# Mamba's weights and phi's fold set among the first experts' blocks, and the opening of Mamba in an order of its own

## The chip, the core and the metric

The kernel is one program on one core of a Trainium2 chip. The metric is device time of one execution in microseconds (us), the median of several runs. PE is TensorE (PEld its weight loads), DVE is VectorE, ACT ScalarE, POOL GpSimd, SP SyncE, which here only issues DMAs.

## The reference

Two layers work on an activation x of 4 x 1024 tokens with 128 features, all in fp32. A layer norm stands ahead of every part, and every part's result is added to x.

```
x = x0                                   # 4 x 1024 x 128
x += MoE(LN(x))                          # 8 experts, top 2, hidden 512, 1024 places each; half weight
x += Mamba(LN(x))                        # inner 256, state 16, causal conv of 4 taps
x += MoE(LN(x))                          # the same experts again; half weight
x += SoftMoE(LN(x))                      # 64 experts x 32 slots, logits x @ phi.T + phi_b
x += GLA(LN(x))                          # 16 heads of 8, gated linear attention
x += SoftMoE(LN(x))

Mamba:  u, z  = split(x @ W_in);   uc = silu(conv4(u) + conv_b)
        dt, B, C = split(uc @ W_xproj)
        delta = softplus(dt @ W_dt + b_dt)
        h_t = exp(-delta_t exp(A_log)) * h_(t-1) + delta_t B_t uc_t
        out = ((sum_n C_t h_t + D uc) * silu(z)) @ W_out
```

## The kernel before

Tokens lie on 128 partitions in 32 tiles of 128 tokens; a "tile group" is four of them, 512 tokens. The stages follow one another:

- **Front and routing** (`front`, `moe_routes`): x is loaded in eight DMAs on SP, each tile group gets its layer norm (DVE statistics, a power on POOL, then `nmr` on DVE), is transposed, and its normed rows `xn_d` go to HBM. DVE ranks the experts and works out each slot's token, `src`, and each result's place, `dest`. SP then loads the experts' weights w1, w2, b2 and clears `y2_d`, the place of results, in HBM (4 MB).
- **First experts** (`moe_experts`): 64 chunks of 128 slots in 16 blocks of four. POOL issues an indirect gather for each chunk, four blocks ahead, and an indirect scatter of each result (L405, L411). For a block, PE transposes (`turn`), multiplies by w1 (`hidden`, ACT evicts with Relu) and by w2 (`output`, DVE evicts to `eo`). The order is written out by hand: `turn(blk + 2)`, `hidden(blk + 1)`, gathers and scatters, `output(blk)`. When no gather is left, POOL does a small memset in its place ("spacer").
- **The fold of phi** (`soft_weights`, L878 to L915), for the much later soft experts: for each of four quarters of phi, ACT squares it, PE sums the squares over the partitions (`pn`) and spreads phi's last row (`pr`), DVE takes the greatest sum and subtracts. Then phi's bias is transposed, its bounds are tested (`flag`), and its negative is put in phi's last row by way of HBM. Here `ones` is a memset on POOL.
- **Opening of Mamba** (`mamba_layer`): weights w_in, w_x, w_dt, w_out and cw (the conv's taps, multiplied into w_in by DVE) are loaded on ACT's queue; A and dg are made. Then come the first half row (512 tokens) of Mamba by `prologue`, and, mixed into it, the results of the first experts by `combine`: for each tile group y is brought from `y2_d` by SP, ACT scales the first choice (L502), DVE multiplies the second and adds x (L494), adds both (L512), and takes the layer norm's statistics (L124, L125, L128), POOL the power (L138), DVE `nmr` (L145). `prologue` transposes the normed tiles (xn, L201; pt, L597), copies them (xT, L599), does the conv and projection as 128x512 matmuls (pu, L618 and L624), evicts (uc, L609; zs, L613), applies Silu to both, projects again (pp, L636; dbc, L641), and makes delta and du (L656 to L680). dbc's rows B and C go by HBM (`bc_d`) to all partitions.
- **Mamba's units**: 8 half rows x 16 states, each a decay on ACT, scans on DVE, products on POOL and sums on PE, in an order by hand. Then the second routing (its constants, `tri_f` to `keep` in `moe_routes`, are made by POOL whenever its memory is free), the second experts with the same code, soft experts, GLA, soft experts.

Within `tc.manual_schedule(engines=ENGINES)` the order on PE, DVE, ACT and POOL is that of the code; SP's and everything outside is placed by a scheduler. Each engine runs its queue in order. `combine` mixes a tile group's pieces into `prologue` three at a time, each group in one go:

```
others = (_ for j in range(4, NT, 4) for _ in pieces(j, wk))
for _ in prologue(*halves[0], rs[0], psa, "dA"):
    for _ in range(3):
        next(others, None)
```

Of the kernel before, what the change touches and what calls it, by code (L numbers as in the profile page):

```python
# [18 lines left out]
P = 128  # L19
B, S, D = 4, 1024, 128  # L20
T = B * S
# [50 lines left out]
def macaron_kernel(ctx: ExitStack, tc: tile.TileContext, a: dict, out: bass.AP):  # L72
# [319 lines left out]
    def moe_experts(w1, w2, b2, tag, xn_d, src, dest):  # L392

        with ExitStack() as s1:
# [64 lines left out]
            with tc.manual_schedule(engines=ENGINES):  # L459
                for c in range(AHEAD * 4):  # L460
                    gather(c)
                turn(0)
                turn(1)
                hidden(0)
                for blk in range(NBLK + 1):
                    if blk + 2 < NBLK:
                        turn(blk + 2)
                    if blk + 1 < NBLK:
                        hidden(blk + 1)
                    for i in range(4):  # L470
                        c = (blk + AHEAD) * 4 + i
                        if c < NSB:
                            gather(c)
                        elif blk > 0:
                            nc.gpsimd.memset(spacer, 0.0)
                        if blk > 0:
                            scatter((blk - 1) * 4 + i)
                    if blk < NBLK:
                        output(blk)

# [49 lines left out]

    def run(pieces):
        for _ in pieces:
            pass


    def mamba_layer(ln, ln_next, first, route, rxp):
# [5 lines left out]
        with ExitStack() as s:  # L542
# [10 lines left out]
            w_in = load("w_in", [D, 2 * DI], wp)  # L553
            w_x = load("w_x", [P, NC, XO[2] + DS], wp)
            w_dt = load("w_dt", [DR, DI], wp)
            w_out = load("w_out", [P, NC, D], wp)
            cw = wp.tile([P, DC, DI], F32, name="cw")
            nc.scalar.dma_start(
                out=cw.rearrange("p k c -> p (k c)"), in_=a["conv_wT"].partition_broadcast(P)
            )  # L560

            for k in range(DC):
                nc.vector.tensor_tensor(cw[:, k, :], cw[:, k, :], w_in[:, :DI], ALU.mult)

            def col(name, c):
                i = COLS[name].start + c
                return cols[:, i : i + 1]

            A = wp.tile([P, NC * DS], F32, name="A")
            nc.scalar.activation(A, cols[:, COLS["A_log"]], AF.Exp)  # L570
            nc.vector.tensor_scalar(A, A, -1.0, None, ALU.mult)
            dg = wp.tile([P, NC, P], F32, name="dg")
            for c in range(NC):
                nc.vector.tensor_scalar(dg[:, c, :], ident, col("D", c), None, ALU.mult)
# [6 lines left out]
            def prologue(b, h, r, ps=ps, tag="mm"):  # L581
# [102 lines left out]
                yield  # L684

# [131 lines left out]
            with tc.manual_schedule(engines=ENGINES):  # L817
                bring, pieces = first
                for j in range(0, 16, 4):
                    bring(j, wk)  # L820
                run(pieces(0, wk))


                others = (_ for j in range(4, NT, 4) for _ in pieces(j, wk))
                for _ in prologue(*halves[0], rs[0], psa, "dA"):
                    for _ in range(3):
                        next(others, None)
                run(others)
                for k in range(3):
                    at(fetch, k)  # L830
                at(feed, 0)
                at(feed, 1)
                at(decay, 0)
                at(decay, 1)
                LEAD = 5
                ahead, old, behind = (iter(()) for _ in range(3))
                for k in range(-LEAD, len(units) + 7):
                    if k % DS == DS - LEAD and (k + LEAD) // DS + 1 < len(rs):
                        i = (k + LEAD) // DS + 1
                        old, ahead = ahead, prologue(*halves[i], rs[i])  # L840
                    if k < 0:
                        next(ahead, None)
                        continue
                    if k > DS and k % DS == 2:
                        behind = epilogue(rs[k // DS - 1])
                    at(fetch, k + 3)
                    at(scan, k)
                    late = next(behind, None)
                    at(keep, k)
                    at(decay, k + 2)  # L850
                    at(times_c, k - 1)
                    at(feed, k + 2)
                    at(sums, k - 2)
                    if late:
                        next(behind)
                    next(old, None)
                    next(ahead, None)
                run(behind)
                route.top_two(NT - NJ, NJ)

# [6 lines left out]
    def soft_weights(pool):  # L867
# [3 lines left out]
        phiN = load("phiT", [D, NS], pool)  # L871
        pbc = pool.tile([P, NSC], F32, name="pbc")
        flag = pool.tile([1, 1], I32, name="flag")
        with (
            tc.tile_pool(name="fold", bufs=2) as wk,
            tc.tile_pool(name="foldp", bufs=2, space=PSUM) as ps,
        ):
            pb = wk.tile([NSC, P], F32, name="pb", bufs=1)  # L878
            nc.scalar.dma_start(out=pb, in_=a["phib"].rearrange("(c p) -> c p", p=P))
            ones = wk.tile([P, P], F32, name="ones", bufs=1)  # L880
            nc.gpsimd.memset(ones, 1.0)
            n2 = wk.tile([P, NS // 512], F32, name="n2", bufs=1)
            for q in range(NS // 512):
                qs = slice(q * 512, (q + 1) * 512)
                sq = wk.tile([P, 512], F32, name="sq")
                nc.scalar.activation(sq, phiN[:, qs], AF.Square)
                pn = ps.tile([P, 512], F32, name="pn")
                nc.tensor.matmul(pn, ones, sq, start=True, stop=True)
                nc.vector.tensor_reduce(n2[:, q : q + 1], pn, AX.X, ALU.max)
                pr = ps.tile([P, 512], F32, name="pr")  # L890
# [4 lines left out]
                nc.vector.tensor_tensor(phiN[:, qs], pr, phiN[:, qs], ALU.subtract)  # L895

            pt = ps.tile([P, 512], F32, name="pt", tag="pn")
            nc.tensor.transpose(pt[:, :NSC], pb, ident[:NSC, :NSC])
            nc.scalar.copy(pbc, pt[:, :NSC])
            ab = wk.tile([P, 1], F32, name="ab", bufs=1)  # L900
# [4 lines left out]
            pc = ps.tile([P, 512], F32, name="pc", tag="pr")  # L905
            nc.tensor.matmul(pc[:, 0:1], ones, ab, start=True, stop=True)
            nm = wk.tile([P, 1], F32, name="nm", bufs=1)
            nc.vector.tensor_reduce(nm, n2, AX.X, ALU.max)
            nc.vector.tensor_scalar(nm, nm, MAX_N2, None, ALU.is_le)
            nc.vector.tensor_tensor(nm, nm, pc[:, 0:1], ALU.add)  # L910
            nc.vector.tensor_scalar(flag, nm[0:1, :], float(P + 1), None, ALU.is_equal)
            nc.scalar.activation(pb, pb, AF.Copy, scale=-1.0)
# [3 lines left out]
        return phiN, pbc, flag  # L916
# [778 lines left out]
    with tc.tile_pool(name="moewa", bufs=1) as wpool:  # L1695
        with tc.tile_pool(name="rtmpa", bufs=1) as tp:
            route = moe_routes("a", tp)
            with (
# [13 lines left out]
                with tc.manual_schedule(engines=ENGINES | {mybir.EngineType.SP}):  # L1712
# [3 lines left out]
                    for j in range(0, NT + 32, 4):  # L1716
# [4 lines left out]
                        if j == NT + 8:  # L1721
                            weights = moe_weights(wpool)
                            clear()
                        if j == NT + 8:
# [3 lines left out]
        moe_experts(*weights, "a", route.xn_d, src, dest)  # L1728

    spool = ctx.enter_context(tc.tile_pool(name="softw", bufs=1, side="right"))  # L1730
    phiN, pbc, flag = soft_weights(spool)
    with tc.tile_pool(name="rtmpb", bufs=1, side="right") as tp:
        route = moe_routes("b", tp)
        with tc.tile_pool(name="rxb", bufs=1) as rxp:
            mamba_layer(lns[1], lns[2], combine(gates[0], lns[1], 4, "hst"), route, rxp)
# [3 lines left out]


# [117 lines left out]
```

## Time and profile before

| what | us |
|---|---|
| median of 3 runs | 2222.7 |
| lowest and highest run | 2218.91, 2224.62 |
| the profiled execution | 2225.24 |
| its span, first to last instruction | 2223.5 |
| front and routing, to the first gather | 0 to 66.1 |
| first experts, to the end of the last scatter | 66.1 to 230.9 |
| opening of Mamba, to du of the first half row | 230.9 to 288.9 |
| Mamba, second routing, to the first gather | 288.9 to 846.6 |

Busy over the whole span: PE 1919.8 us (86%), DVE 1397.4 (63%), ACT 952.3 (43%), POOL 1399.0 (63%). The mean granted clock of PE is 0.927 of full speed. A row of the timeline gives start, duration, engine, line, operation, output<-inputs, size, and in brackets the idle time of the engine before it and what ended that. A row of a table by stage gives the stage's bounds and length, each engine's busy time and count, the granted clock as a share of full speed, the share of time that the DMA engines were busy, and GB/s.

### The profile page before, as it was taken

Reading aid. Unit: us, or ns where it says so; the run is one execution under the profiler, and the core shown is the slowest. Engines: PE = TensorE matmul, PEld = TensorE weight load, DVE = VectorE, ACT = ScalarE, POOL = GpSimd, SP = SyncE. Lnnn points to the kernel's source line nnn. Section 1 sums busy time; section 2 is a strip of 40 time slices with the busy share of each in tenths; the row PEclk is TensorE's granted clock in tenths of the full one; section 3 lists DMA queues with packets and bytes.
Section 4 is the critical chain, followed back from the end, with each engine's and each line's share of the span. In section 5 each row is a group of like instructions: output and inputs, shape, how many; then the busy total and the mean of one; then the engine's idle time right before and its main releaser. Section 6 shows DMA issues by size and latency. Waiting matters only on the chain. (4 is left out here: it accounts for less than half of the span.)

```text
span 2223.5 us, 18016 instructions
## 1 busy us (share of the span) xinstructions
PE 1919.8 (86%) x5893; PEld 892.6 (40%) x5893; DVE 1397.4 (63%) x1839; ACT 952.3 (43%) x1595; POOL 1399.0 (63%) x919
## 2 busy tenths in 40 slices
PE   5788578888999866885999989997888999989998
PEld 3556223333334324653444444443223344434443
DVE  6211678888888982115888645566976788744445
ACT  4322466677776623222443343332542333333331
POOL 3677278898988946775555566662543455556663
PEclk9999789999899876997999999998987999999999
DMA  7111433332332324112000000000000000000000
GB/s 248 49 52 50 143 107 98 107 117 101 124 105 98 116 95 129 52 51 63 19 10 0 1 1 1 0 1 6 1 0 1 1 0 1 1 1 5 10 10 16
DMA packets 63389, 110.70 MB, mean 50 GB/s; under 512 B 7967, under 2 KB 41391, under 8 KB 58293
## 3 DMA queue, kind: packets, MB, share of 16 engines
q1 hardware_dynamic: 53222, 85.04, 11.6%
q0 software_dynamic: 8192, 16.79, 2.7%
q10 hardware_dynamic: 1874, 7.65, 1.0%
q8 instruction: 48, 0.79, 0.2%
q14 instruction: 53, 0.43, 0.1%
HBM read 90.00 MB, written 19.44 MB: 49 GB/s over the span
## 5 line engine op out<-in xcount | busy, mean ns | idle before, releaser
L1017 POOL TENSOR_TENSOR dm<-ex,sm 128x1024 f32<-128x1024 f32 x128 | 247.8, 1936 | 215.2 <-DVE sm L1013 109.1
L758 POOL TENSOR_TENSOR hc<-hst,Cs 128x1024 f32<-128x1024 f32 x127 | 280.9, 2220 | 55.2 <-DVE hst L741 24.9
L1125 POOL TENSOR_TENSOR acc<-acc,L 128x1024 f32<-128x1024 f32 x96 | 226.0, 2355 | 116.6 <-ACT L L1117 115.9
L773 PE MATMUL py<-hc,ident 128*128 128x512 f32 x512 | 278.1, 674 | 17.6 <-POOL hc L758 17.4
L1117 ACT ACTIVATE L<-pl,pbc 128x512 f32<-128x512 f32 x256 | 162.1, 684 | 283.7 <-PE pl L1107 273.2
L1005 ACT ACTIVATE ex<-l,nmh 128x1024 f32<-128x1024 f32 x128 | 142.7, 1115 | 289.9 <-DVE nmh L1000 269.7
L996 PE MATMUL l<-phiT,xT 128*128 128x512 f32 x512 | 247.8, 608 | 18.8 <-ACT ex L1005 15.6
L1107 PE MATMUL pl<-xT,phiM 128*128 128x512 f32 x512 | 244.7, 603 | 0.1
L1151 PE MATMUL py<-L,yt 128*128 128x512 f32 x512 | 238.4, 593 | 4.4 <-DVE L L1141 4.4
L1028 PE MATMUL px<-dm,xn 128*128 128x512 f32 x512 | 240.8, 593 | 1.1 <-POOL dm L1017 1.1
L1000 DVE TENSOR_REDUCE nmh<-l 128x1 f32<-128x1024 f32 x128 | 156.1, 1220 | 78.8 <-PE l L996 78.2
L731 ACT ACTIVATE dA<-delta,A 128x512 f32<-128x512 f32 x256 | 177.1, 719 | 50.8 <-DVE hst L741 45.7
L437 ACT ACTIVATE hT<-ph,cols 128x512 f32<-128x512 f32 x128 | 88.0, 687 | 216.5 <-PE ph L433 216.5
L723 POOL TENSOR_TENSOR dBu<-du,Bs 128x1024 f32<-128x1024 f32 x78 | 172.5, 2212 | 1.7 <-DVE du L680 1.2
L741 DVE TENSOR_TENSOR_SCAN hst<-dA,carry,dBu 128x512 f32<-128x512 f32 x128 | 155.4, 1264 | 11.8 <-ACT dA L731 6.3
L773 PEld LDWEIGHTS py<-hc,ident 128*128 128x128 f32 x512 | 96.2, 202 | 163.5 <-issue 122.0
L996 PEld LDWEIGHTS l<-phiT,xT 128*128 128x128 f32 x512 | 97.9, 194 | 150.7 <-issue 116.8
L741 DVE TENSOR_TENSOR_SCAN hst<-dA,dBu 128x512 f32<-128x512 f32 x128 | 147.5, 1203 | 16.9 <-POOL dBu L723 8.5
L1012 DVE TENSOR_REDUCE sm<-ex 128x32 f32<-128x1024 f32 x128 | 154.7, 1209 | 0.0
L452 DVE TENSOR_TENSOR eo<-po,b 128x512 f32<-128x512 f32 x32 | 22.1, 692 | 207.6 <-PE po L447 207.6
L411 POOL DMA_INDIRECT y_d<-eo,dest x128 | 126.1, 985 | 40.9 <-issue 25.6
L1151 PEld LDWEIGHTS py<-L,yt 128*128 128x128 f32 x512 | 96.8, 190 | 127.3 <-issue 117.0
(259 smaller groups left out, 3016.6 us busy)
## 6 DMA issues: line engine op xcount, KB each, us to landing
Cs<-bc_d SPq DMA_DIRECT2D x32, 1024.0 KB, 5.9
Bs<-bc_d SPq DMA_DIRECT2D x78, 256.0 KB, 3.1
w<-in_w SPq DMA_DIRECT2D x4, 2048.0 KB, 8.2
y<-y_d SPq DMA_DIRECT2D x32, 256.0 KB, 3.3
y_d<-zero SPq DMA_DIRECT2D x1, 4096.0 KB
ew<-in_ew ACTq DMA_DIRECT2D x1, 4096.0 KB
x<-in_x SPq DMA_DIRECT2D x8, 256.0 KB, 6.9
xn_da<-xr SPq DMA_DIRECT2D x8, 256.0 KB, 4.9
```

What stands on the lines that cost most here:

```text
L723: eng.tensor_tensor(dBu, r["du"], r.pop(("B", n)).unsqueeze(2).to_broadcast([P, HB, NC]), ALU.mult,)
L731: nc.scalar.activation(dA, r["delta"][:, :, c], AF.Exp, scale=A[:, c * DS + n : c * DS + n + 1],)
L741: nc.vector.tensor_tensor_scan(hst[:, :, c], r.pop(("dA", n, c)), dBu[:, :, c], 0.0 if h == 0 else carry[b][:, c, n : n + 1], ALU.mult, AL ...
L758: eng.tensor_tensor(hc, r.pop(("h", n)), Cs.unsqueeze(2).to_broadcast([P, HB, NC]), ALU.mult)
L773: nc.tensor.matmul(r["py"][:, c, :], ident, hc[:, :, c], start=False, stop=(n == DS - 1))
L996: nc.tensor.matmul(l[:, q * 512 : (q + 1) * 512], xT[:, j * P : (j + 1) * P], phiN[:, o : o + 512], start=True, stop=True,)
L1017: nc.gpsimd.tensor_tensor(dms[k], exs.pop(k), sms.pop(k).unsqueeze(2).to_broadcast([P, NG, PS]), ALU.mult,)
L1028: nc.tensor.matmul(px[hf * 2 + q], xns[j // 4][:, j % 4, :], dmf[:, q * 512 : (q + 1) * 512], start=(j == 0), stop=(j == NT - 1),)
L1107: nc.tensor.matmul(pl[:, i, :], phiM[:, (2 * c + i) * P : (2 * c + i + 1) * P], xT[:, t * TB : (t + 1) * TB], start=True, stop=True,)
L1117: nc.scalar.activation(L[:, i, :], pl[:, i, :], AF.Exp, bias=pbc[:, 2 * c + i : 2 * c + i + 1], scale=-1.0,)
L1125: nc.gpsimd.tensor_tensor(accs[t], accs[t], L, ALU.add)
L1151: nc.tensor.matmul(pys[t], yt[:, 2 * c + i, :], L[:, i, :], start=(c + i == 0), stop=(c == CS - 1 and i == 1),)
```

## The change

Three things change, all ahead of Mamba's units.

1. phi and Mamba's weights are loaded by SP right after the clearing of `y2_d` (phi was loaded on ACT's queue at the start of the kernel, Mamba's weights there at its opening). Their tiles have pools of their own on the other side of SBUF. The fold and the making of cw, A and dg become generators, whose pieces `moe_experts` runs one by one after `output(blk)` from block 2 on: four quarters of phi (blocks 2 to 5), the bias and bounds (6), the flag and the row by HBM (7), cw (8), A and dg (9). The fold's PSUM tiles come from the ring of `ph`. `ones` is made by DVE.
2. The first half row has `opening` in place of `prologue`: uc and zs are evicted from PSUM with Silu at once, the second z projection comes after pp, and each step follows the former without empty pieces between.
3. In place of `combine`, `flow` brings the results of the first experts: the scale of the next tile group is issued ahead of the present group's add, and `nmr` of a group comes behind the next group's add. (The second experts' results still use `combine`.)

In the program as built, two more things follow. From du of the first half row on, each engine's order is that of before. The eleven instructions of POOL that make the second routing's constants, which stood behind the first tile group's power, now stand behind the gather of chunk 52 and ahead of the scatter of chunk 32: their pool now shares addresses with the fold's tiles.

```diff
@@ moe_experts
+                others = extra(psh, "ph") if extra else iter(())
                 for blk in range(NBLK + 1):
...
                     if blk < NBLK:
                         output(blk)
+                    if blk >= 2:
+                        next(others, None)
+    def flow(gate, ln, yp, tag):
...
+        def scale(j):
+            if j < NT:
+                for i in range(4):
+                    nc.scalar.activation(
+                        ys[j][:, 0, i, :], ys[j][:, 0, i, :], AF.Copy,
+                        scale=gate[:, 0, j + i : j + i + 1],
+                    )
+        def add(j):
+            y = ys.pop(j)
...
+            bring(j + 16)
+        for j in range(0, 16, 4):
+            bring(j)
+        scale(0)
+        add(0)
+        ln_group(ln, 0)
+        yield
+        scale(4)
+        for j in range(4, NT, 4):
+            scale(j + 4)
+            add(j)
+            yield
+            if j > 4:
+                ln_minus(ln, j - 4)
+            ln_stats(ln, j)
+            ln_pow(ln, j)
+            yield
+        ln_minus(ln, NT - 4)
+    def mamba_weights(wp):
+        w = {
+            "w_in": load("w_in", [D, 2 * DI], wp, nc.sync),
...
+        def pieces():
+            for k in range(DC):
+                nc.vector.tensor_tensor(
+                    cw[:, k, :], cw[:, k, :], w["w_in"][:, :DI], ALU.mult
+                )
+            yield
...
+            def opening(r, ps, tag):
...
+                def project(q):
...
+                        nc.scalar.activation(uc[:, q, :], pu, AF.Silu, bias=col("conv_b", q))
...
+                        nc.scalar.activation(zs[:, q - NC, :], pu, AF.Silu)
+                for q in range(NC + 1):
+                    project(q)
+                    yield
...
+                project(NC + 1)
+                yield
...
-                bring, pieces = first
-                for j in range(0, 16, 4):
-                    bring(j, wk)
-                run(pieces(0, wk))
-                others = (_ for j in range(4, NT, 4) for _ in pieces(j, wk))
-                for _ in prologue(*halves[0], rs[0], psa, "dA"):
-                    for _ in range(3):
+                others = first(wk, "hst")
+                next(others)
+                for i, _ in enumerate(opening(rs[0], psa, "dA")):
+                    next(others, None)
+                    if i % 2:
                         next(others, None)
                 run(others)
@@ soft_weights
-        phiN = load("phiT", [D, NS], pool)
+        phiN = load("phiT", [D, NS], pool, nc.sync)
...
-            nc.gpsimd.memset(ones, 1.0)
+            nc.vector.memset(ones, 1.0)
...
@@ macaron_kernel
+    spool = ctx.enter_context(tc.tile_pool(name="softw", bufs=1, side="right"))
+    mpool = ctx.enter_context(ExitStack())
+    mwp = mpool.enter_context(tc.tile_pool(name="mwts", bufs=1, side="right"))
+    with (
+        tc.tile_pool(name="moewa", bufs=1) as wpool,
+        tc.tile_pool(name="fold", bufs=1, side="right") as fp,
+    ):
...
                             clear()
+                            phiN, pbc, flag, fold = soft_weights(spool)
+                            mweights, made = mamba_weights(mwp)
...
+        def extra(ps, tag):
+            yield from fold(fp, ps, tag)
+            yield from made()
+        moe_experts(*weights, "a", route.xn_d, src, dest, extra)
```

## The prediction

> **What bounds the kernel now.** I read the table by stage first, to see which stage the change touches and what limits it.
>
> ```profile
> core 0: us, PE busy (x) PEld busy (x) DVE busy (x) ACT busy (x) POOL busy (x), PEclk, DMA share, GB/s
> 0.00:66.00 66.00, 34.24 (x162) 26.09 (x162) 41.26 (x140) 25.61 (x60) 22.08 (x49) 1.00 0.62 216
> 66.00:231.00 165.00, 136.75 (x710) 93.23 (x710) 23.15 (x34) 45.13 (x66) 127.37 (x149) 0.95 0.18 51
> 231.00:290.00 59.00, 27.26 (x47) 10.29 (x47) 41.03 (x144) 31.72 (x64) 10.32 (x13) 0.64 0.52 162
> ```
>
> Stage 66 to 231 is the first experts, 231 to 290 the opening of Mamba. In the opening no engine is full: it is a chain of waits. In the experts' stage POOL shows 127 of 165 us, but the timeline of POOL has it issuing gathers and scatters from 66.14 to 230.87 with nothing but 0.3 us between two of them (and one hole of 1.1 at 211), one every 1.28 us. POOL sets that stage's end; ACT and DVE are mostly idle there, and PE waits 24.8 us for gathers. The timeline around the change:
>
> ```profile
> 8.21 0.29 DVE L124 BATCH_NORM_STATS2 st<-x 128x6 f32<-128x128 f32 x1 [0.81 <-DMA x<-in_x]
> ...
> 229.90 0.97 POOL L411 DMA_INDIRECT y_d<-eo,dest  x1 [0.19 <-issue]
> ...
> 232.16 2.59 SPq L491 DMA_DIRECT2D y<-y_d  x5
> ...
> 244.71 0.16 DVE L145 SCALAR_TENSOR_TENSOR nmr<-mv,rstd 128x4 f32<-128x4 f32 x1 [1.16 <-POOL rstd L138]
> ...
> 248.80 0.56 ACT L599 COPY xT<-pt 128x512 f32<-128x512 f32 x1
> ...
> 258.41 0.69 ACT L609 ACTIVATE uc<-pu,cols 128x512 f32<-128x512 f32 x1 [1.58 <-PE pu L618]
> ...
> 287.61 1.26 DVE L680 TENSOR_TENSOR du<-delta,uc 128x1024 f32<-128x1024 f32 x1
> ```
>
> Call S the start of the last scatter, 229.90. From S the opening reaches its marks at +14.8 (first tile group's nmr), +18.9 (xT copy), +28.5 (second uc), +57.7 (du). From du on, the order of instructions on every engine is the same in both kernels, so what is won up to du is won in the end. The same first steps occur without a fold beside them after the second experts, whose last scatter starts at 1014.45:
>
> ```profile
> 1014.45 0.97 POOL L411 DMA_INDIRECT y_d<-eo,dest  x1 [0.19 <-issue]
> ...
> 1019.79 1.28 ACT L502 ACTIVATE y<-y,gate 128x128 f32<-128x128 f32 x4 [18.14 <-DMA y<-y_d]
> 1020.52 1.14 DVE L494 SCALAR_TENSOR_TENSOR y<-y,gate,x 128x128 f32<-128x128 f32 x4 [10.88 <-DMA y<-y_d]
> ...
> 1025.61 0.16 DVE L145 SCALAR_TENSOR_TENSOR nmr<-mv,rstd 128x4 f32<-128x4 f32 x1 [1.23 <-POOL rstd L138]
> ```
>
> There nmr stands at +11.2 from the scatter, not +14.8. That is my template for the new opening.
>
> **The opening (flow, opening, weights made earlier), step by step from S.**
> nmr +11.2; the first xn 0.2 later, +11.4. ACT still runs eight scales of y (tile groups 4 and 8) behind xn and ahead of the xT copy: 1.55 after xn's start plus 2.34 (246.46 to 248.80 in the row of before) gives the xT copy at +15.3; before +18.9.
> The second uc came 9.6 after the xT copy (258.41 against 248.80); the matmuls between are the same 16 passes: +24.9. I add 0.75 for the clock (below): +25.65. Silu now evicts directly, and its table load (1.28) stands in ACT's queue ahead of the first uc, where ACT waits for PE anyway, so it leaves the path.
> Meanwhile DVE does seven further tile groups without waiting for POOL's power. From rows of one group: four multiply-adds 1.22, add to stats 0.73, stats to eps 1.9, nmr 0.1: 3.9 a group, where before the nmr rows stand 5.05 apart, 1.12 of it idle until POOL's power, as in front of the nmr above. The one place where the new order still stops DVE is the group at 16: its scales (1.26) are behind the second uc on ACT. 25.65 + 0.7 + 1.26 puts that add at +27.7 (DVE alone would be there at +25.9). Three more groups of 3.9: +39.4; last stats 2.7: +42.1; power and nmr 1.3: +43.4; then w, l and delta, 1.25 each (282.16 to 283.41): du at +47.2. ACT's own chain from there: second uc 0.7, four groups of scales 5.0, two Silu evictions 1.4, dbc 0.6, four evictions of pd 2.8 (the 2.15 from dbc to the first of them, 268.62 to 270.78, is filled by scales and a Silu but for 0.2), then 5.9 from the last to the end of Ln (274.44 to 280.35): +42.3, inside DVE's +43.4. B and C fetches start about +31 and have 10 us to spare. Gain of the opening: 57.7 - 47.2 = **10.5 us**.
>
> The clock. In the windows 249:253 and 253:257 the granted clock is 0.50 and 0.99: the first 3.6 us of these matmuls run at half speed, 0.85 a pass for 0.43. After the second experts, where PE had idled longer (no fold before it), the first eight passes all took 0.83 (6.66 us). The fold no longer runs just ahead, so I take 5.1 us at half speed, the middle between 3.6 and 6.7: half of the difference, +0.75. Bounds: 0, and all 16 passes slow, +4.7.
> [...]
>
> **The fold and the weights among the blocks.** Each quarter of phi adds to PE four passes of 0.43 (1.7), to ACT one square (0.63), to DVE 0.69 twice; the first also waits about 1.1 for ones, now a DVE memset behind eo. The small rest, cw (4 x 0.42), A and dg are some 4 us of DVE in all. The cover is POOL's pace: eo of block 2 ends at 106.86 and its scatter goes at 113.29, 6.4 us later; from block 3 on the lead is 9 to 13. The pieces add at most 2.8 + 3 x 1.7 = 8 us to PE by block 5, spread over four blocks, and PE waits 1.5 to 2.5 per block for gathers later, which give it back. I cost them at nothing; without cover they would cost those 8 us.
> POOL's own queue: the set-up of the second routing (tri_f to keep, eleven instructions) was at 7.16 to 9.23, in idle time. Its pool now lies over the fold's tiles, and the order puts it behind the gather of chunk 52 and ahead of scatter 32, near 175 us, where POOL is the bound: **+2.1**. Queued behind it are all later gathers and scatters, so S moves with it. Bounds: 1.0 (the hole at 211 takes up 1.1 of it) and 3.3 (a wait and an issue gap more). Its wait is for the fold's last reads, due about 20 us earlier.
>
> **The loads.** phi (1 MB) left ACT's queue at 1.73 and shared the DMA engines with x; DVE lost 0.81 waiting for the second x group (row above). It now follows w1, w2, b2 and the clearing: **-0.8** (0 to -1), since from there to the first gather it is one chain. The 2 MB moved behind the clearing extend traffic that ended near 57 us by some 5 us at its 400 GB/s, before the first gather at 66. SP has nothing left between scatters and y loads except the flag, read earlier. pb on SP waits for nothing late.
>
> **Sum.** -10.5 + 2.1 - 0.8 = -9.2 us. The profiled execution took 2225.24 us (span 2223.5), so 2216.0 for it; it lies 2.5 above the median of 2222.7, which gives **2213.5 us**.
>
> **Rivals.**
> *The opening wins little* (0.17). PE stays slow through all 16 passes and pp and pd after them, so that ACT's in-order scales hold up DVE at 16, 20 and 24: 4.7 less, and about 1 more at pp. For it: ACT is in order, and a scale stands behind every eviction. Against it: before, the clock rose 3.6 us into the same matmuls. Gain 10.5 - 5.7 = 4.8, less 1.3 net upstream: -3.5, 2219.2.
> *POOL stands still in the middle of the experts* (0.05), the one that ends slower. The set-up's first memset waits for the fold's last read; if phi arrived late (it is behind 8.5 MB), the fold would stall PE at block 2 and POOL at chunk 52. The fold spans blocks 2 to 7, about 46 us (106 to 152). It decides once the wait passes the 9.2 won: the fold would have to end after 184, so phi to land after 138 instead of near 62. If it landed at 150, the fold would end at 196, POOL would wait 21 us, and the time be 2213.5 + 21 = 2234. Against it: DMA is 18% busy in that stage.
> *More is won* (0.10): the hole at 211 swallows half of the set-up (1.1), and the clock rises so early that the scales at 16 come in time (1.8): -12.1, 2210.6.
> The forecast has 0.68.
>
> **Numbers.** By its own bounds (set-up 1.0 to 3.3, x 0 to -1, clock 3.6 to 6.7 us) the forecast spans 2211.5 to 2216.5; for 8 in 10 the range reaches to the two near rivals: 2208.5 to 2219.5. 0.3% is 6.7 us, about what a measurement of this kernel tells from no change: faster means under 2216.0. That takes nearly all of the forecast and of the third rival, 0.76; same 0.19; slower 0.05.
>
> **What would show it.** Right: first gather near 65.3; last scatter near 231.2 with tri_f to keep inside POOL's row near 174; nmr at S + 11.2, xT at S + 15.3, du at S + 47; every later mark 9 earlier. Wrong: S later than 233, a wait in front of tri_f, scatters waiting for eo, granted clock at 0.5 beyond 7 us of pu, or DVE idle in front of more than one add.

## The result, and the profile after

The changed kernel takes **2216.76 us** (median of 20 runs, 2210.57 to 2222.43) against 2223.59 for the kernel before (20 runs beside them, 2218.91 to 2227.32): a ratio of 0.9968, 95% interval 0.9958 to 0.9977, or 6.8 us won, between 5.1 and 9.3. The forecast was 9.2 won; the 6.8 are just past the 6.7 that it named as about the least that can be told from no change. The profiled execution of the changed kernel is one of its slower ones, 2221.28 us with a span of 2219.1, only 4.0 under that of the kernel before. So there are two things to explain: what was won where the change is, and why the end shows less.

One fact is needed for the numbers below: e1 to e4 ran on chip 10 and e9 to e12 on chip 4, and on both every kernel took 40 to 50 us longer (the kernel before: 2269.7 and 2271.7). They are called the long chips here. e5 to e8 ran on chip 9 (the kernel before: 2224.9) and agree with the first two profiles, whose chip is not on record; the chips of these six profiles are called the short chips. Times are compared only within a series; marks are counted from S, the start of the last scatter of the first experts.

The table by stage of the changed kernel, cut at its first gather and its last scatter:

```profile
core 0: us, PE busy (x) PEld busy (x) DVE busy (x) ACT busy (x) POOL busy (x), PEclk, DMA share, GB/s
65.00:231.00 166.00, 135.94 (x723) 93.86 (x723) 29.77 (x54) 46.55 (x71) 128.01 (x158) 0.98 0.18 51
231.00:280.00 49.00, 16.97 (x34) 6.77 (x34) 33.93 (x125) 27.31 (x57) 10.12 (x13) 0.60 0.56 176
```

The experts' stage holds 6.6 us more of DVE and no less of POOL, and is not shorter; the opening has shrunk from 59 to 49 us. The timeline of the changed kernel at the places shown for the kernel before, and at the new ones:

```profile
7.33 0.28 DVE L124 BATCH_NORM_STATS2 st<-x 128x6 f32<-128x128 f32 x1
...
172.51 0.97 POOL L407 DMA_INDIRECT g<-xn_da,src  x1 [0.30 <-issue]
173.48 0.22 POOL masks.py:65 MEMSET tri_f<- 128x128 f32 x1
...
175.40 0.13 POOL L232 MEMSET keep<- 128x8 f32 x1
176.12 1.02 POOL L413 DMA_INDIRECT y_d<-eo,dest  x1 [0.59 <-issue]
...
231.03 0.97 POOL L413 DMA_INDIRECT y_d<-eo,dest  x1 [0.19 <-issue]
...
242.39 0.16 DVE L145 SCALAR_TENSOR_TENSOR nmr<-mv,rstd 128x4 f32<-128x4 f32 x1 [1.16 <-POOL rstd L138]
...
245.44 0.69 DVE L564 TENSOR_TENSOR x<-y 128x512 f32<-128x512 f32 x1 [1.84 <-ACT y L552]
...
246.48 0.56 ACT L769 COPY xT<-pt 128x512 f32<-128x512 f32 x1
...
247.14 9.93 PE L778 MATMUL pu<-xT,cw 128*128 128x512 f32 x16 [2.38 <-ACT xT L769]
...
257.11 0.69 ACT L782 ACTIVATE uc<-pu,cols 128x512 f32<-128x512 f32 x1 [2.75 <-PE pu L778]
...
258.99 0.69 DVE L564 TENSOR_TENSOR x<-y 128x512 f32<-128x512 f32 x1 [2.37 <-ACT y L552]
...
277.84 1.25 DVE L833 TENSOR_TENSOR du<-delta,uc 128x1024 f32<-128x1024 f32 x1
```

DVE no longer waits for x at the start. The set-up of the second routing stands in POOL's row with no wait in front: from the gather at 172.51 to the scatter at 176.12 are 3.61 us instead of 1.28. S is 231.03; nmr comes at S + 11.4, the xT copy at S + 15.45, the second uc at S + 26.1, the add of group 16 at S + 28.0, du at S + 46.8. In the kernel before du stood at S + 57.7. So at du the changed kernel is 9.77 us ahead, and at the end of the span 4.4. From du on both kernels run the same instructions in the same order (but for one last nmr of DVE, which the kernel before has behind du), yet the changed one took 1941.2 us for them and the other 1935.9.

### The profile page after: what moved, and what is told of

Read it like the earlier page. It is cut to its first block, busy times and chain, and to the rows that moved or that the text cites. A ratio compares the mean times of both kernels' runs of the same rounds, so it can differ in the third digit from the quotient of the medians.

```text
span 2219.1 us, 17996 instructions
## 1 busy us (share of the span) xinstructions
PE 1896.7 (85%) x5893; PEld 886.4 (40%) x5893; DVE 1400.1 (63%) x1840; ACT 949.5 (43%) x1593; POOL 1396.3 (63%) x918
## 5 line engine op out<-in xcount | busy, mean ns | idle before, releaser
L1293 DVE TENSOR_TENSOR L<-L,rd 128x1024 f32<-128x1024 f32 x128 | 147.0, 1211 | 0.1
```

## Experiments

The table gathers all profiles; each column is worked out from the starts of the instructions named. "Mamba" is du to the first gather of the second experts, "experts 2" from there to their last scatter, "soft 1" the first to the last pass of l, the soft experts' logits, "GLA" from there to the first pass of l in the second soft experts. "Half" is the time in GLA at half granted clock, by the clock records of the trace.

| profile | first gather | S | S to du | Mamba | experts 2 | soft 1 | GLA | half |
|---|---|---|---|---|---|---|---|---|
| before | 66.14 | 229.90 | 57.71 | 558.96 | 167.88 | 236.06 | 460.34 | 76.0 |
| before, e5 | 65.29 | 228.71 | 56.56 | 558.57 | 167.46 | 236.04 | 456.38 | 57.7 |
| after | 65.20 | 231.03 | 46.81 | 558.21 | 169.45 | 237.36 | 463.89 | 78.9 |
| e6 set-up free | 65.29 | 228.78 | 46.29 | 558.17 | 169.41 | 237.75 | 460.14 | 75.8 |
| e7 scales early | 65.22 | 231.04 | 42.69 | 558.44 | 167.63 | 236.06 | 456.08 | 57.7 |
| e8 warm | 65.21 | 232.02 | 54.28 | 557.76 | 169.81 | 237.75 | 459.95 | 76.0 |
| *chip 10:* e1 after | 65.14 | 254.90 | 45.51 | 557.24 | 191.14 | 236.05 | 457.29 | 69.3 |
| e2 old opening | 65.26 | 254.31 | 54.11 | 557.79 | 190.38 | 237.72 | 459.87 | 76.0 |
| e3 fold behind | 65.30 | 258.63 | 47.12 | 557.48 | 189.94 | 237.74 | 460.13 | 75.9 |
| e4 both repairs | 65.24 | 253.57 | 42.75 | 555.83 | 188.74 | 236.05 | 459.89 | 76.1 |
| *chip 4:* e9 after | 65.30 | 255.17 | 46.64 | 558.38 | 189.87 | 237.35 | 463.08 | 81.5 |
| e10 fold behind | 65.42 | 255.65 | 46.97 | 559.97 | 191.29 | 236.05 | 463.97 | 78.9 |
| e11 both repairs | 65.44 | 253.40 | 43.12 | 557.66 | 189.90 | 237.75 | 457.26 | 69.3 |
| e12 warm, gated | 65.30 | 255.09 | 45.37 | 557.43 | 188.63 | 237.75 | 463.98 | 78.9 |

**Is the loss behind du the kernel's, or the execution's? (e1, e9, e5.)** No edit: the changed kernel twice more, the kernel before once.

> The changed kernel once more, nothing edited. The first profile had du at 277.84, 9.8 us ahead of the kernel before, but the span ended only 4.4 ahead: from du to the end it took 1941.3 us against 1935.9. Theory A (clock windows): what lies behind du is the same instructions, and the loss is the luck of the granted clock, which drops by half for windows of 3.41 us and takes 1.7 us of a TensorE-bound stretch each time. Then first gather, last scatter and du repeat within 0.3 us (65.2, 231.0, 277.8), the stretch from du to the end does not (anything from 1932 to 1944), and the two profiles of this one kernel drift apart behind du in steps near 1.7 us where their clock records differ. Theory B (the new order costs something later): the stretch from du to the end repeats at 1941.3 within 1 us, with the same steps at the same places.

> The changed kernel once more, as the measure for the three others of this call. On a chip like the first: first gather 65.2, S 231.0, du at S + 45.5 to 46.8 (its two profiles), and a stretch from the last pass of the first soft experts to the first pass of the second that lies anywhere from 456 to 464 (463.9 in its first profile, 457.3 in its second, 456.4 to 460.3 in the two of the kernel before): by the theory of clock windows it does not repeat; by the rival (a lasting cost of the new order) it is 463 or more on the chip where it was 463.9.

> The kernel before, nothing edited, for a profile beside those of this call. The chip of the runs e1 to e4 was slower for every kernel (before: 2269.7), by about 24 us in each experts' stage, where TensorE showed gaps of issue between its passes; marks are therefore counted from S, the last scatter. Expected: S to du 57.7 within 1 us, whatever the chip; from du to the end, outside of the second experts' stage, the same as in every other run but for steps of 1.7.

Measured: e1 2259.43 us, ratio 0.9947 (0.9926 to 0.9967); e9 2263.88, 0.9967 (0.9948 to 0.9985); e5 2225.54, 1.0003 (0.9992 to 1.0014). First gather and S to du of the changed kernel repeat within 1.3 us, not within the 0.3 that was expected, and S itself moves with the chip. What follows du does not repeat (e1's 1954.0 from du to the end holds a second experts' stage 21.7 longer). The stretch GLA of the changed kernel took 463.9, 457.3 and 463.1 us, that of the kernel before 460.3 and 456.4, with the same instructions. One row over that stretch, of the first profile and of e1:

```profile
1257.00:1721.00 464.00, 416.46 (x1326) 172.43 (x1324) 296.98 (x372) 176.84 (x289) 242.67 (x124) 0.91 0.00 1
```

```profile
1299.00:1757.00 458.00, 413.36 (x1327) 168.99 (x1326) 295.88 (x373) 177.04 (x289) 242.60 (x124) 0.92 0.00 1
```

DVE, ACT and POOL have the same work to 1.1 us; PE is busy 3.1 us longer at a lower clock. Over the 14 profiles the stretch goes with its time at half clock (the last two columns): 456 us where 57.7 us are at half, 457 at 69.3, 460 to 464 at 76 and above. It is no price list: from 57.7 to 69.3 the stretch grows by 1.1, from 76.0 to 78.9 by 3.8. In the clock records of the first profiles of both kernels every stretch at one clock, but for the last, which the end of the record cuts, is a multiple of 3.41 us long (3.41 to 249.17 us, each at 1.00 or 0.50); 3.41 us are called a window here. The weight loads of pu's passes in the first profile of the changed kernel start 0.85 us apart up to 252.83, where the record has 0.50, and 0.43 apart behind it, where it has 1.00; by these numbers one window at half clock costs a PE that is busy all through it an estimated 1.7 us of work. The stretch soft 1 takes one of three values, 236.05, 237.35 and 237.75. Held against each other instruction by instruction, the first two profiles of the changed kernel drift apart and back between du and the second experts by up to 6.5 us, mostly in steps of 1 to 3, as the first profiles of the two kernels do. Theory B, a fixed loss of GLA, falls with e1's 457.3 and, on the short chips, with the 456.1 of e7, which from du on is the same. Of theory A it is shown that the stretch does not repeat; that the clock is the cause is argued. Which comes first in each place, the longer time or the half clock, the columns do not tell. Two counts even speak against theory A for the whole: from du to the end the first profile of the kernel before has 270 us at half clock and that of the changed one 248, though the latter took longer; and over the 20 runs of the changed kernel, time and mean granted clock do not go together (correlation -0.07). These counts hold half windows in which PE had no work as well, so they are rough.

From the first pair, the 5.3 us lost behind du are: Mamba -0.75, experts 2 +1.57, soft 1 +1.30, GLA +3.55, and -0.3 in the rest. A small lasting cost is not excluded: on the short chips, du to the end took 1935.9 and 1931.5 with the order before (mean 1933.7) and 1941.2, 1937.9, 1931.7 and 1937.4 with the new ones (1937.1).

e5 also shows what the forecast could not see, in the timeline of the kernel before's second profile:

```profile
7.34 0.29 DVE L124 BATCH_NORM_STATS2 st<-x 128x6 f32<-128x128 f32 x1
...
228.71 0.97 POOL L411 DMA_INDIRECT y_d<-eo,dest  x1 [0.19 <-issue]
```

phi's load is still at the front there, and the 0.81 us of waiting for x is not: the first gather is at 65.29.

**Which half of the change won the 10.9? (e2, e3, e10.)** e2 keeps fold and weights among the blocks and takes the old order of the opening (lines shortened):

```
-  lambda yp, tag: flow(gates[0], lns[1], yp, tag)
+  combine(gates[0], lns[1], 4, "hst")
-  others = first(wk, "hst"); next(others)
-  for i, _ in enumerate(opening(rs[0], psa, "dA")):
-      next(others, None)
-      if i % 2: next(others, None)
+  bring, pieces = first
+  for j in range(0, 16, 4): bring(j, wk)
+  run(pieces(0, wk))
+  others = (_ for j in range(4, NT, 4) for _ in pieces(j, wk))
+  for _ in prologue(*halves[0], rs[0], psa, "dA"):
+      for _ in range(3): next(others, None)
```

> Fold and weights stay among the blocks; the opening goes back to the old order (combine and the general prologue). It tells how much of the 10.9 us won between last scatter and du (57.7 to 46.8) is the missing fold and weights, and how much the order. My theory: last scatter S stays at 231.0; first nmr at S + 11.4 instead of S + 14.8, because only the fold and the weights stood in its way; the rest of the old opening is unchanged, so du at S + 54 (285): 3.4 won by moving the fold, 7.2 by the order. Time about 7 us above the changed kernel, near 2224. Rival (the order does nothing, the freed DVE does it all): du at S + 47 to 48, time within 1 us of the changed kernel. Second rival (the fold was hidden behind other waits): nmr S + 14.8, du S + 57.7, time near 2228.

Measured: 2270.13 us, ratio 1.0003 (0.999 to 1.0017): nothing of the gain is left, and the time is 10.7 above e1, where 7 was expected. From its timeline:

```profile
254.31 0.97 POOL L413 DMA_INDIRECT y_d<-eo,dest  x1 [0.19 <-issue]
...
265.52 0.16 DVE L145 SCALAR_TENSOR_TENSOR nmr<-mv,rstd 128x4 f32<-128x4 f32 x1 [1.16 <-POOL rstd L138]
...
272.33 0.16 DVE L145 SCALAR_TENSOR_TENSOR nmr<-mv,rstd 128x4 f32<-128x4 f32 x1 [1.14 <-POOL rstd L138]
...
277.38 0.16 DVE L145 SCALAR_TENSOR_TENSOR nmr<-mv,rstd 128x4 f32<-128x4 f32 x1 [1.12 <-POOL rstd L138]
...
308.42 1.25 DVE L751 TENSOR_TENSOR du<-delta,uc 128x1024 f32<-128x1024 f32 x1
```

nmr at S + 11.2 and du at S + 54.1, both as expected: beside the old order, fold and weights out of the way are worth 3.0 (57.1, the mean of the two profiles of before, less 54.1). Groups still stand 5.05 apart, with 1.12 of waiting for POOL's power in each; in the changed kernel the adds of two groups without a wait stand 3.75 apart. And 3.0 less the 2.25 that POOL's set-up costs (e6, on a short chip) is no gain that these runs can tell.

e3 and e10 are one kernel, the opposite half: the new opening, with phi's fold behind the experts again (shortened).

```
-  moe_experts(*weights, "a", route.xn_d, src, dest, extra)
+  moe_experts(*weights, "a", route.xn_d, src, dest)
+with (tc.tile_pool(name="fold", bufs=1) as fp,
+      tc.tile_pool(name="foldp", bufs=4, space=PSUM) as fps):
+    for _ in extra(fps, "ph"): pass
```

> The opposite half: the new order of the opening stays, but phi's fold and the products of the weights go back behind the experts (the loads stay where the change put them, and POOL's set-up of the second routing is early again, because nothing lies under its tiles). My theory: S at 228.7 (231.0 less the 2.3 of the set-up); DVE, ACT and TensorE have the fold ahead of the first group, so nmr at S + 14.8 and du at S + 50.2 (279): about 1.4 later than in the changed kernel, time near 2218. Rival (the new order has slack that swallows the fold): du at S + 47, time near 2214.5.

> The kernel of e3 again (phi's fold behind the experts, loads and opening as in the changed kernel; the products of the weights are placed early by the scheduler, near 78, as e3 showed). On the slow chip du came at S + 47.1, because fold and first y tile hardly meet: from the end of the experts' last eo DVE, ACT and TensorE wait about 12 for y, and only 1.3 of the fold falls behind y's landing. My theory now: on a chip like the first, S at 228.8 (no set-up in POOL's row), du at S + 47.1, so near 275.9, about 1.5 ahead of the changed kernel: moving the fold among the blocks costs 2.3 on POOL and brings 0.8. Time 1.5 under that of e9, so equal to it by the measurement. Rival (the fold among the blocks is worth the 3 that it brought beside the old order, 57.1 to 54.1): du at S + 49, 278 or later.

Measured: e3 2262.67 us, 0.9964 (0.9949 to 0.998); e10 2262.49, 0.996 (0.9942 to 0.9978), e9 beside it 2263.88. du is at S + 47.1 and S + 47.0, not at S + 50.2: e3's number was a miss by 3, and its rival's (S + 47) came. The timeline of e10 tells why:

```profile
249.31 0.69 DVE L454 TENSOR_TENSOR eo<-po,b 128x512 f32<-128x512 f32 x1 [2.88 <-issue]
...
250.10 0.17 DVE L1029 MEMSET ones<- 128x128 f32 x1
...
251.88 0.69 DVE L1037 TENSOR_REDUCE n<-pn 128x1 f32<-128x512 f32 x1 [1.62 <-issue]
...
255.65 0.97 POOL L413 DMA_INDIRECT y_d<-eo,dest  x1 [0.19 <-issue]
...
257.03 0.69 DVE L1037 TENSOR_REDUCE n<-pn 128x1 f32<-128x512 f32 x1
261.84 0.35 DVE L560 SCALAR_TENSOR_TENSOR y<-y,gate,x 128x128 f32<-128x128 f32 x1 [4.12 <-DMA y<-y_d]
262.11 0.68 DVE L1043 TENSOR_TENSOR phiT<-pr,phiT 128x512 f32<-128x512 f32 x1
```

Between the last eo and the first y DVE has 12 us to wait, and the fold lies in them but for its last 1.3 us. The kernel before has that gap too, from its last eo at 222.56 to its first add of y at 238.96, but there the fold fills the end of it:

```profile
230.87 0.22 POOL L881 MEMSET ones<- 128x128 f32 x1
...
231.15 5.26 PE L888 MATMUL pn<-sq,ones 128*128 128x512 f32 x6 [4.74 <-POOL ones L881]
```

In the kernel before `ones` is a memset of POOL, queued behind the last scatter, so the fold's sums begin at S + 1.25. In e10 DVE makes `ones` right behind the last eo, and they begin at S - 4.9 (250.72). So e3 and e10 put the fold back but not the engine of `ones`, and the fall from 3.0 to 0.7 is not the new order's alone; the kernel before with this one memset moved was not run.

With `ones` on DVE and the new order, then, the fold's move among the blocks brings 0.7 at du (46.3, the mean of after, e1, e9 and e6, against 47.0) and costs 2.25 on POOL. That this half alone would be 1.5 ahead of the whole change on the short chips is worked out from these marks; it was run on the long chips only, where S moves by up to 5 us from profile to profile and the times do not tell it apart. (The products of the weights did not move behind: the scheduler placed them near 78.)

**What does POOL's set-up cost, and what do the scales on ACT? (e6, e7, e4, e11.)** e6 lays the fold's tiles on the other side of SBUF, so that the constants of the second routing no longer wait for them:

```
-        tc.tile_pool(name="fold", bufs=1, side="right") as fp,
+        tc.tile_pool(name="fold", bufs=1) as fp,
```

> The first of the two repairs of e4 alone: POOL makes the constants of the second routing at the start. My theory: the set-up costs 2.3 where POOL's issue of gathers and scatters is the bound. On a chip like that of the first profiles S is at 228.7 (changed kernel 231.0), the time 2.3 lower, near 2214.5. On a chip like that of e1 to e4, POOL waits for eo in front of nine scatters, and the set-up falls into such a wait: S and the time as in the changed kernel, within 1. S to du stays at 45.5 to 47. Rival (the set-up was hidden in the 1.3 us hole before the last scatters): S unchanged on either chip.

Measured: 2211.93 us, 0.9941 (0.9924 to 0.9957). Its timeline:

```profile
7.21 0.20 POOL masks.py:65 MEMSET tri_f<- 128x128 f32 x1
...
228.78 0.97 POOL L413 DMA_INDIRECT y_d<-eo,dest  x1 [0.19 <-issue]
```

These are four runs, and the changed kernel was not run beside them. tri_f is back in POOL's idle time, and S is 2.25 earlier (231.03 in the changed kernel, 231.04 in e7 on the same chip as e6). From first gather to S are 163.5 us, in the two profiles of before 163.76 and 163.42: the fold itself costs the experts nothing on a short chip. What was expected for a long chip was not run alone; in e4 and e11 S is 1.3 and 1.8 ahead of e1 and e9, but e3 and e10, one kernel, have S 3.0 apart there.

e7 issues the scales a tile group earlier, into ACT's wait for the first nmr:

```
         scale(0)
+        scale(4)
+        scale(8)
         add(0)
...
-        scale(4)
         for j in range(4, NT, 4):
-            scale(j + 4)
+            scale(j + 8)
```

> The second repair of e4 alone: scales of y a group earlier on ACT. S as in the changed kernel; S to du 42.8 as in e4 (42.75), 3.3 under the mean of the two profiles of the changed kernel (46.8 and 45.5); no idle of DVE in front of an add. Time about 3 lower than the changed kernel. Rival (part of e4's gain from S to du came from POOL's earlier constants): 45 or more.

Measured: 2210.91 us, 0.9953 (0.9935 to 0.997), again from four runs. Its timeline:

```profile
238.58 1.28 ACT L552 ACTIVATE y<-y,gate 128x128 f32<-128x128 f32 x4 [1.23 <-DMA y<-y_d]
240.78 1.28 ACT L552 ACTIVATE y<-y,gate 128x128 f32<-128x128 f32 x4 [0.92 <-DMA y<-y_d]
242.49 1.65 ACT L201 ACTIVATE xn<-x,nmr,rstd 128x128 f32<-128x128 f32 x4 [0.44 <-DVE nmr L145]
...
243.60 0.69 DVE L564 TENSOR_TENSOR x<-y 128x512 f32<-128x512 f32 x1
...
254.86 0.69 DVE L564 TENSOR_TENSOR x<-y 128x512 f32<-128x512 f32 x1
...
273.73 1.26 DVE L834 TENSOR_TENSOR du<-delta,uc 128x1024 f32<-128x1024 f32 x1
```

Both waits of DVE are gone (the adds of groups 4 and 16, 243.60 and 254.86), and du is at S + 42.7. The add of group 16 stands at S + 23.8. ACT waits 0.92 for y of group 8, and these scales end 0.4 before xn: a landing later by more than that would hold xn.

e4 and e11 carry both edits.

> Two repairs of the changed kernel. One: the fold's tiles lie on the other side of SBUF, not under the constants of the second routing, so POOL makes these constants at the start and not between two scatters: S at 228.7, 2.3 earlier. Two: the scales of the tile groups 4 and 8 are issued in the 4.8 us in which ACT waits for the first nmr, and every later one a group earlier. In the changed kernel the scales behind xn hold the xT copy from S + 13.9 (transposes done) to S + 15.45, and DVE stands 1.84 in front of the add of group 4 and 2.37 in front of that of group 16. My theory: xT copy S + 13.9, no idle of DVE in front of an add, du at S + 43 (between 42.6 and 44.8), so near 272 and 6 us ahead of the changed kernel; time near 2211. Rival (ACT's chain to the end of Ln takes the place of DVE's): du at S + 45.5, time 2213. Rival on the other side (y of group 8 lands late and holds ACT ahead of xn): xn later than S + 12, du no earlier than S + 47.

> The kernel of e4 again, for a chip like the first: S at 228.8 as in e6, du at S + 42.7 as in e4 and e7, so near 271.5; time 5.6 under that of e9. Rival (the two repairs overlap): du at 273 or later, 3 to 4 under e9.

Measured: e4 2254.73 us, 0.9936 (0.9912 to 0.9959), e1 beside it 2259.43; e11 2259.29, 0.9943 (0.9923 to 0.9963), e9 beside it 2263.88. S to du 42.75 and 43.12; du at 296.52 in e11, 301.81 in e9, 5.3 earlier, and 4.6 in the times; against e1, e4 is 4.1 earlier at du and 4.7 in the times. This version is faster than the kernel before. That it beats the changed kernel shows plainly at du; in the times both series agree on it, but their runs overlap. On the short chips it was not run; there its halves gave 2211.93 and 2210.91.

**What does the half clock at the start of pu cost? (e8, e12.)** Both add products on PE whose results are not used. e8: eight of y of group 12 ahead of the transposes, four behind them; e12: two of group 0's new x ahead, one behind. The edit of e12, shortened:

```
+  wm = psa.tile([P, HB], F32, name="wm", tag="dA")
+  for _ in range(2): nc.tensor.matmul(wm, ident, x0, start=True, stop=True)
   for i, _ in enumerate(opening(rs[0], psa, "dA")):
+      if i == 0: nc.tensor.matmul(wm, ident, x0, start=True, stop=True)
```

> The changed kernel with twelve more passes of TensorE over a tile of y (results unused): eight before the first transposes and four behind them, so that TensorE is busy from about S + 7 to the first pu. It tests the term for the clock. In the two profiles of the changed kernel the 16 passes of pu took 9.93 and 8.77 us (5.7 and about 3.5 us of them at half clock), DVE's wait in front of the add of group 16 was 2.37 and 1.20, and du stood at S + 46.8 and + 45.5: 1.2 us all three. My theory: with the clock full all 16 passes take 6.9, the wait is 0 and du at S + 44.3. Rival (the extra passes hold the transposes, or the clock stays at half through them): xT copy later than S + 16, pu 9 or more, du at S + 46 or later.

> The extra passes of e8 stood too late: y of group 12 landed at S + 13, and the passes held the transposes back by 11 us; but the pu passes behind them took 7.03 in place of 8.8 to 9.9. Now three products of group 0's new x (two ahead of the transposes, ready at S + 8.3, and one behind them) keep TensorE busy from S + 8.4 to S + 15.4. My theory: transposes and xT copy stay at S + 12.1 and S + 15.3, pu takes 7.0, DVE's wait in front of the add of group 16 goes from 1.2 to 2.4 down to nothing, du at S + 44.4, time 1 to 2 under e9. Rival (the clock needs more than 7 us of passes to come back): pu 8.7 or more, du at S + 45.5 or later.

Measured: e8 2225.67 us, 1.0001 (0.9991 to 1.0011); e12 2262.42, 0.9954 (0.9935 to 0.9973). e8 went the rival's way: y of group 12 landed at S + 13, so the extra passes held the transposes until 254.62. Its passes of pu:

```profile
245.00 9.78 PE L978 MATMUL wm<-y,ident 128*128 128x512 f32 x16 [19.34 <-DMA y<-y_d]
254.62 0.60 PE L768 MATMUL pt<-ident,xn 128*128 128x128 f32 x4
255.05 3.60 PE L981 MATMUL wm<-y,ident 128*128 128x512 f32 x8
258.49 7.03 PE L779 MATMUL pu<-xT,cw 128*128 128x512 f32 x16
```

They take 7.03 us, 0.44 each, near the spacing of 0.43 that loads at 1.00 had above; in after, e1, e9, e6, e7 and e11 they took 9.93, 8.77, 10.04, 9.74, 8.75 and 9.89. With the scales early this matters little: pu took 1.1 longer in e11 than in e7, and du came 0.4 later (S + 43.12, 42.69). In e12 nothing was held, but pu was no faster than in e1 or e7:

```profile
263.18 3.75 PE L977 MATMUL wm<-x,ident 128*128 128x512 f32 x4 [14.44 <-DVE x L564]
266.87 1.48 PE L767 MATMUL pt<-ident,xn 128*128 128x128 f32 x4
268.19 1.02 PE L980 MATMUL wm<-x,ident 128*128 128x512 f32 x2
270.87 8.80 PE L778 MATMUL pu<-xT,cw 128*128 128x512 f32 x16 [1.66 <-issue]
```

The table by stage of e12 for the window of the clock ahead of pu and the next, and for two windows later on (the clock is the column behind POOL):

```profile
267.57:270.98 3.41, 1.70 (x6) 0.64 (x6) 1.71 (x6) 3.41 (x12) 0.00 (x0) 1.00 0.14 33
270.98:274.39 3.41, 3.41 (x5) 1.33 (x6) 3.15 (x15) 2.26 (x5) 1.05 (x1) 0.50 0.51 152
...
366.55:369.97 3.42, 1.68 (x4) 0.68 (x4) 3.42 (x4) 2.02 (x5) 3.27 (x2) 1.00 0.00 0
369.97:373.38 3.41, 3.41 (x9) 1.15 (x7) 3.41 (x4) 3.20 (x6) 3.41 (x3) 1.00 0.30 72
```

The granted clock was full from 267.57 to 270.98, one window, and half again in the next, behind 1.66 us of idle ahead of pu. du stayed at S + 45.4. It is a miss, and its rival's number (pu 8.7 or more) is right for another reason than it gave: the clock had come back, and was lost again. What keeps it is not shown: the window at 366.55 was as little busy (1.68 us), and the clock stayed. So a du at full clock was not measured in either run; the price of 1.2 us is worked out from the profiles whose pu differ.

## Why the prediction was right, and where not

**The total** held: the 2216.76 lie in the range, 3.3 above the 2213.5. By the marks 8.7 were won instead of 9.2 (below), the median shows 6.8, and the statement about the end was wrong.

**The opening, -10.5**: measured -10.9 between the first profiles, and -10.8 between the means (57.1 and 46.3). Its marks came within 0.5 us: nmr + 11.4 for + 11.2, xT + 15.45 for + 15.3, second uc + 26.1 for + 25.65, add of group 16 + 28.0 for + 27.7, du + 46.8 for + 47.2. The step in it that failed is "the one place where the new order still stops DVE is the group at 16". DVE also stood 1.84 us in front of the add of group 4, because the eight scales behind xn were charged to the xT copy alone. It cost nothing then, since the add of group 16 waits for ACT in any case, so that the first stop only shortens the second; e7 shows that the two together were worth 3.6. "DVE alone would be there at +25.9" was too late as well: without either stop that add stands at S + 23.8 (e7). DVE idle ahead of more than one add was also named as a sign against the forecast; it appeared, and the sum held all the same.

**The clock in it**: 5.1 us at half speed were taken; the profiles with this order show 5.7, 3.35, 5.9 and 5.3. The slow part is not the same in each execution of one kernel (5.7, 3.35 and 5.9 in after, e1 and e9). In the first profile the clock record has 0.50 from 228.93 to 252.83, and PE stood idle from 223.69 to 243.13 ahead of the transposes. DVE's wait at group 16 and du follow it: between after and e1, pu differs by 1.16 us, the wait by 1.17 and du by 1.3. A side effect was overlooked: in the kernel before the four passes of pp ran at half clock (3.70 us, behind 4.21 of idle PE), in the new order at full clock (1.88).

**The attribution.** The text ascribed nmr's 3.6 to fold and weights; e2 agrees at nmr and gives 3.0 at du beside the old order, and e10 only 0.7 for the fold beside the new one. Most of the gain is the order's: 7.8 of the 10.8 come on top of fold and weights (54.1 to 46.3). The fold needed no move among the blocks to be nearly hidden: 10.1 (57.1 to 47.0) come without it, from the order, the early weights and `ones` on DVE, which no run takes apart. What the text did not see is that `ones`, on POOL behind the last scatter, is what the fold waited for (4.74 us of PE, and 4.80 in e5).

**POOL's set-up, +2.1**: +2.25 (e6), with no wait ahead of tri_f. The hole behind it stayed (1.28 us ahead of the scatter at 213.20), so the lower bound of 1.0 had no ground.

**The fold hidden at no cost**: shown by e6 on a short chip.

**The loads, -0.8**: the mark (first gather 65.20) is right and the reason is not. The wait of 0.81 belonged to one of two executions; e5 has phi's load at the front and its gather at 65.29. That the mark came true was luck. The term should have been 0 to -0.8 with 0 more likely. The sum is then -10.8 + 2.25 - 0.1 = -8.7, inside the measured 5.1 to 9.3.

**"Every later mark 9 earlier"** failed at the end: 9.8 at du, 8.9 at the last scatter of the second experts, 9.1 and 7.8 at the first and last pass of l in the first soft experts, 3.7 at the last pass of PE. The step under it, that what is won up to du is won in the end, does not hold for one pair of profiles: GLA alone moves by 8 us between executions of the same instructions. The runs of the changed kernel span 12 us; the cause was not shown. Whether the 2 us between 8.7 and the measured 6.8 are luck or a small lasting cost stays open.

**The rivals.** "The opening wins little": of the 8.8 to 10.0 us of pu 3.3 to 5.9 were at half clock, pp and pd ran at full clock, and du of the changed kernel never came later than S + 46.8. "POOL stands still": no wait ahead of tri_f. "More is won": the hole did not swallow the set-up.

## What to carry to other kernels

Cost a reordering by marks against a local event, and treat the stretch behind it as noise until several profiles of one kernel say otherwise (here GLA took 456 to 464 us). A wait that is seen in one profile may be that execution's alone: ask whether another profile repeats it before it becomes a term. Before work is moved out of a gap, look whether the gap ends with it or with a transfer, and whether one small instruction of it stands late in another engine's queue (here `ones`); and when a pool is moved, look at which engine's queue inherits what lay under it, since here one word (the side of SBUF) was worth 2.25 us on POOL and the scales' order 3.6 us on DVE, together half of what the whole opening won.

## What was not expected of the hardware

**The clock was halved behind a window that was only half idle.** In e12 PE was busy for the first 1.6 us of a window of 3.41 and idle for the rest, and the next window was granted 0.50 (270.98 to 274.39, above). It is no rule: 0.8 of these 1.6 us were transposes (pt), and another window of the same run that was half idle kept the clock (366.55, above). What tells the two apart stays open.

**On two chips TensorE waits between its passes in the experts.** On the long chips both experts' stages of the changed kernel were 20 to 24 us longer (e1 and e9 against its first profile), and every kernel profiled there was long in them. The timeline of PE in e1, in block passes that take 3.73 us in the first profile without a gap:

```profile
155.50 2.95 PE L449 MATMUL po<-w,hT 128*128 128x128 f32 x25
158.69 0.46 PE L449 MATMUL po<-w,hT 128*128 128x128 f32 x2 [0.24 <-issue]
160.07 0.27 PE L449 MATMUL po<-w,hT 128*128 128x128 f32 x1 [0.92 <-issue]
...
162.17 0.37 PE L449 MATMUL po<-w,hT 128*128 128x128 f32 x1 [1.04 <-issue]
163.56 0.37 PE L449 MATMUL po<-w,hT 128*128 128x128 f32 x1 [1.02 <-issue]
```

PE waits up to 1 us ahead of these passes for nothing that the profile shows (no such gap above 0.2 us stands in the first experts of the six profiles of the short chips), and POOL then waits for eo ahead of its scatters (21.3 us in nine waits in e1), so that POOL's row no longer sets the end of the stage. The cause was not tried.
